# Input projection by seven block products in place of eight, with a short convolution over 1024 tokens

## Chip, cores, metric

The kernel runs on one core of a Trainium2 chip, in float32 throughout. The metric is the device time of one execution in microseconds (us). Engines are named as in the profile: PE (TensorE, matrix products), PEld (its weight loads), DVE (VectorE), ACT (ScalarE), POOL (GpSimd), SP (SyncE, which issues most transfers).

## What is computed

The reference is one layer of a long-convolution mixer and a mixture of experts over 8192 tokens of 512 channels. The part that matters here is its beginning, `x` of [8192, 512] and `W_in` of [512, 1536]:

```python
u = x @ W_in + b_in                              # [8192, 1536]
uc = short_conv(u, short_w, short_b)             # three taps: tokens t-2, t-1, t
x0, x1, v = split(uc, 3)                         # 512 channels each
gate = v * x1
taps = gen_filter(8192, W1, b1, f1, W2, b2, f2, W3, b3)   # small network with sines, times a decay
y = (long_conv(gate, taps) + filter_bias) * x0
x = layernorm(x + y @ W_out + b_out)
# then: experts chosen by a maximum over groups of 32 tokens, two products, layernorm
```

`x` is also read by the projection in a transposed copy, `xT` of [512, 8192].

## The kernel before

There are three stages one after another: `project`, `convolve` and `experts`. Only `project` is changed. It computes `u`, the short convolution and the gate, and beside that the filter's taps, and writes `x0`, `gate` and `taps` to DRAM, from where `convolve` reads them.

The projection works on one block of 512 tokens (`TB`, 16 blocks) and one group of 128 channels (`ct`, four groups) at a time, in `projection(b, ct)`. Its three streams `s` are `x0`, `x1` and `v`. For each stream four matmul calls (over the 512 input channels, `k`) fill one PSUM bank (L260). A call is two records in the profile. ACT then copies the bank to SBUF with the bias added (`u`, L269) and makes the last tap of the short convolution from it (`o`, L271); DVE adds the other two taps (L272, then L277, or for `x0` two halves in another order of tokens, L283). The last two columns of `u` are carried to the next block by two small copies on POOL (L253, L286). POOL multiplies `gate` (L288), and SP stores `x0` (L289) and `gate` (L293).

Between projections stand the pieces of the filter, called `rides`: 16 pieces with sines (`filter_1`, `filter_2`, `sine`, L197 to L203: seven DVE instructions and one of ACT for 512 columns), then 32 pieces that make the taps (`some_taps`: eight small exponentials on ACT at L238, two PSUM adds on DVE at L241, two products on POOL at L245). They are spread evenly over the 64 projections:

```python
upto = len(rides) * (b * NCT + ct + 1) // slots
for f, *args in rides[done:upto]:
    f(*args)
```

PSUM has eight banks, which all these share in turn. Engine orders in this stage are made by the framework's scheduler from the program's order and its modelled durations; a queue then runs its instructions strictly in that order, and semaphores make an instruction wait for what it reads and for the buffer that it writes. Token loads (`load_tokens`, L161) go through SP into two buffers.

Of the kernel before, what the change touches and what calls it, by code (L numbers as in the profile page):

```python
# [13 lines left out]
F32 = mybir.dt.float32  # L14
# [81 lines left out]
@with_exitstack  # L96
def hyena_then_experts(ctx: ExitStack, tc: tile.TileContext, i: dict, out: bass.AP):
    nc = tc.nc

    const = ctx.enter_context(tc.tile_pool(name="const", bufs=1))  # L100
    dram = ctx.enter_context(tc.tile_pool(name="dram", bufs=1, space=bass.MemoryType.DRAM))

    def load(pool, name):
        t = pool.tile(list(i[name].shape), F32, tag=name, name=name + "_sb")
        nc.sync.dma_start(out=t, in_=i[name])
        return t

    ident = const.tile([P, P], F32, tag="ident", name="ident")
    make_identity(nc, ident)

    def in_dram(what, shape):
        return [dram.tile(shape, F32, tag=f"{what}{ct}", name=f"{what}{ct}") for ct in range(NCT)]


    y_dram = {
        (ct, n): dram.tile([P, BT], F32, tag=f"y{ct}_{n}", name=f"y{ct}_{n}")
        for ct in range(NCT)
        for n in range(NBLK)
    }


    with tc.tile_pool(name="pairs", bufs=2) as pairs, tc.tile_pool(name="in", bufs=3) as tables:
        kept = {
            name: const.tile(list(i[name].shape), F32, tag=name, name=name + "_sb")
            for name in ("chan", "c_in", "c_back")
        }
        between = in_dram("x0", [P, L]), in_dram("gate", [P, P, N2]), in_dram("taps", [P, P, N2])
        with tc.tile_pool(name="psum1", bufs=8, space=bass.MemoryType.PSUM) as psum:

            def bank(name):  # L130
                return psum.tile([P, 512], F32, tag="ps", name=name)

            project(tc, i, bank, load, between, kept)
        with tc.tile_pool(
            name="psum2", bufs=4, space=bass.MemoryType.PSUM, reuse_waits="tile"
        ) as psum:

            def banks(name):
                return psum.tile([P, 1024], F32, tag="ps", name=name)

            convolve(tc, i, banks, kept, pairs, tables, between, y_dram)
    experts(tc, i, load, ident, y_dram, out)


def project(tc, i, bank, load, between, kept):


    nc = tc.nc
    x0_dram, gate_dram, taps_dram = between
    with tc.tile_pool(name="pr1", bufs=1) as hp, tc.tile_pool(name="pr2", bufs=2) as wk:  # L150

        win = [hp.tile([P, NCT, 3, P], F32, tag=f"win{ct}", name=f"win{ct}") for ct in range(NCT)]

        def load_win(ct):
            come = i["W_in"].rearrange("(k p) (s t c) -> k t p s c", p=P, s=3, c=P)
            for k in range(NCT):
                nc.sync.dma_start(out=win[ct][:, k], in_=come[k, ct])

        def load_tokens(b):
            xt = wk.tile([P, NCT, TB], F32, tag="xt", name=f"xt_{b}")  # L160
            nc.sync.dma_start(  # L161
                out=xt, in_=i["xT"][:, b * TB : (b + 1) * TB].rearrange("(k p) t -> p k t", p=P)
            )
            return xt


        xt = wk.tile([P, NCT, TB], F32, tag="xt", name="xt_0")
        for k in range(NCT):
            nc.sync.dma_start(
                out=win[0][:, k],  # L170
                in_=i["W_in"].rearrange("(k p) (s t c) -> k t p s c", p=P, s=3, c=P)[k, 0],
            )
            nc.sync.dma_start(out=xt[:, k], in_=i["xT"][k * P : (k + 1) * P, 0:TB])
        pe = load(hp, "pe")
        w1 = load(hp, "W1p")
        w2 = load(hp, "W2p")
        bf = load(hp, "bf")
        chan = kept["chan"]
        nc.sync.dma_start(out=chan, in_=i["chan"])
        for ct in range(1, NCT):  # L180
            load_win(ct)
        w3 = load(hp, "W3p")
        b3 = load(hp, "b3b")
        negt = load(hp, "negt")
# [2 lines left out]
            nc.sync.dma_start(out=kept[name], in_=i[name])  # L187

        h2 = hp.tile([P, L // 2], F32, tag="h2", name="h2")
        carry = hp.tile([P, NCT, 3, 2], F32, tag="carry", name="carry")  # L190
        nc.gpsimd.memset(carry, 0.0)

        def sine(dst, ps, layer, name):
            a = wk.tile([P, 512], F32, tag="a", name="a" + name)
            n = wk.tile([P, 512], F32, tag="n", name="n" + name)
            b_ap, f_ap = bf[:, 2 * layer : 2 * layer + 1], bf[:, 2 * layer + 1 : 2 * layer + 2]
            nc.vector.tensor_scalar(a, ps, b_ap, f_ap, ALU.add, ALU.mult)  # L197
            nc.vector.tensor_scalar(n, a, 1.0 / (2 * math.pi), ROUND, ALU.mult, ALU.add)
# [6 lines left out]
        h1s = {}  # L205

        def filter_1(j):
            ps = bank(f"pf1_{j}")
            nc.tensor.matmul(ps, w1, pe[:, bass.ts(j, 512)], start=True, stop=True)
            h1s[j] = wk.tile([P, 512], F32, tag="h1", name=f"h1_{j}")  # L210
            sine(h1s[j], ps, 0, f"0_{j}")

# [7 lines left out]
        def some_taps(ct, j):  # L220
# [11 lines left out]
                    )  # L232
            for half in range(2):
                n2 = half * N2 // 2 + 4 * j
                ex = wk.tile([P, 4, P], F32, tag="ex", name=f"ex_{ct}_{n2}")
                kb = wk.tile([P, 4, P], F32, tag="kb", name=f"kb_{ct}_{n2}")
                for q in range(4):
                    nc.scalar.activation(  # L238
                        ex[:, q, :], delta[:, chans], AF.Exp, scale=negt[:, n2 + q : n2 + q + 1]
# [8 lines left out]
            if j == N2 // 8 - 1:  # L248
                nc.sync.dma_start(out=taps_dram[ct], in_=taps.pop(ct))

        def projection(b, ct):
            u = wk.tile([P, 3, TB + 2], F32, tag="u", name=f"u_{ct}_{b}")
            nc.gpsimd.tensor_copy(u[:, :, 0:2], carry[:, ct])  # L253
            got = []
            pss = [bank(f"pu_{ct}_{b}_{s}") for s in range(3)]
            steps = [(s, k) for s in range(3) for k in range(NCT)]
            if b == 0 and ct == 0:
                steps.sort(key=lambda sk: sk[1])
            for s, k in steps:
                nc.tensor.matmul(  # L260
                    pss[s], win[ct][:, k, s, :], xt[:, k, :], start=(k == 0), stop=(k == NCT - 1)
                )
            for s in range(3):

                def ch(what):
                    at = (s * NCT + ct) * 5 + what
                    return chan[:, at : at + 1]

                nc.scalar.activation(u[:, s, 2:], pss[s], AF.Identity, bias=ch(0))  # L269
                o = wk.tile([P, TB], F32, tag=f"o{s}", name=f"o{s}_{ct}_{b}")  # L270
                nc.scalar.activation(o, u[:, s, 2:], AF.Identity, bias=ch(1), scale=ch(4))  # L271
                nc.vector.scalar_tensor_tensor(  # L272
                    o, u[:, s, 1 : 1 + TB], ch(3), o, ALU.mult, ALU.add
                )
                first = u[:, s, 0:TB]
                if s:
                    nc.vector.scalar_tensor_tensor(o, first, ch(2), o, ALU.mult, ALU.add)  # L277
                    got.append(o)
                    continue
                got.append(wk.tile([P, 2, TB // N2, N2 // 2], F32, tag="o", name=f"o_{ct}_{b}"))  # L280
                first, o = (v.rearrange("p (a h b) -> p h a b", h=2, b=N2 // 2) for v in (first, o))
                for h in range(2):
                    nc.vector.scalar_tensor_tensor(  # L283
                        got[0][:, h], first[:, h], ch(2), o[:, h], ALU.mult, ALU.add
                    )
            nc.gpsimd.tensor_copy(carry[:, ct], u[:, :, TB : TB + 2])  # L286
            gate = wk.tile([P, TB], F32, tag="gate", name=f"gate_{ct}_{b}")
            nc.gpsimd.tensor_tensor(gate, got[2], got[1], ALU.mult)  # L288
            nc.sync.dma_start(  # L289
                out=x0_dram[ct].rearrange("c (h n) -> c h n", h=2)[:, :, b * TB // 2 : (b + 1) * TB // 2],  # L290
                in_=got[0].rearrange("c h a b -> c h (a b)"),
            )
            nc.sync.dma_start(  # L293
                out=gate_dram[ct][b * TB // N2 : (b + 1) * TB // N2].rearrange("a c b -> c a b"),
                in_=gate.rearrange("c (a b) -> c a b", b=N2),
            )


        rides = []
# [1 line left out]
        for j in range(nf):  # L301
            rides += [(filter_1, j)]
            if j:
                rides += [(filter_2, j - 1)]
        rides += [(filter_2, nf - 1)]
        rides += [(some_taps, ct, j) for ct in range(NCT) for j in range(N2 // 8)]

        slots = NTB * NCT - 2
        done = 0
        for b in range(NTB):  # L310
            if b:
                xt = load_tokens(b)
            for ct in range(NCT):
                projection(b, ct)
                upto = len(rides) * (b * NCT + ct + 1) // slots
                for f, *args in rides[done:upto]:
                    f(*args)
                done = max(done, upto)


CC = 16
# [659 lines left out]
```

## Time and profile before

| what | value |
|---|---|
| time, median of 3 runs | 2325.26 us (2318.59 to 2327.2) |
| the profiled execution: time, span | 2320.76 us, 2319.0 us |
| mean granted TensorE clock | 0.969 of full speed |
| busy: PE, DVE, ACT, POOL | 2152.6, 1297.3, 823.7, 478.2 us |
| `project`, first matmul to the first of `convolve` | 4.83 to 724.38 us |
| matmul records of L260, weight loads | 1536, of 592 ns at the median; 190 ns |

The busy time of an engine is the union of its instructions' durations. Matmuls are pipelined: the 592 ns of one overlap with the next, so the rate is to be read from the distance of their starts. Idle time of an engine "before" an instruction is put down to what ended it, the releaser. A mean duration that is longer than the median says that some instructions of the group were held up while they ran.

### The profile page before, as it was taken

Reading aid. Unit: us, or ns where it says so; the run is one execution under the profiler, and the core shown is the slowest. Engines: PE = TensorE matmul, PEld = TensorE weight load, DVE = VectorE, ACT = ScalarE, POOL = GpSimd, SP = SyncE. Lnnn points to the kernel's source line nnn. Section 1 sums busy time; section 2 is a strip of 40 time slices with the busy share of each in tenths; the row PEclk is TensorE's granted clock in tenths of the full one; section 3 lists DMA queues with packets and bytes.
Section 4 is the critical chain, followed back from the end, with each engine's and each line's share of the span. In section 5 each row is a group of like instructions: output and inputs, shape, how many; then the busy total and the mean of one; then the engine's idle time right before and its main releaser. Section 6 shows DMA issues by size and latency. Waiting matters only on the chain. (4 is left out here: it accounts for less than half of the span.)

```text
span 2319.0 us, 65860 instructions
## 1 busy us (share of the span) xinstructions
PE 2152.6 (93%) x29664; PEld 1474.7 (64%) x29664; DVE 1297.3 (56%) x1872; ACT 823.7 (36%) x1248; POOL 478.2 (21%) x583
## 2 busy tenths in 40 slices
PE   9999999999999999999999998889988999888765
PEld 3444444444446999999999998355555556555643
DVE  5677544554544553463463463456566666656647
ACT  4444555555553321231321221121343234224433
POOL 1111333333331340250250160211100100110000
PEclk9999999999999999999999999999998999899887
DMA  5222224232414655655564574526654754665373
GB/s 167 68 64 76 70 65 167 87 136 64 141 59 168 204 172 192 194 199 183 184 219 174 165 245 167 154 77 195 216 193 136 230 185 137 194 217 188 118 264 121
DMA packets 197057, 362.62 MB, mean 156 GB/s; under 512 B 79132, under 2 KB 118946, under 8 KB 193698
## 3 DMA queue, kind: packets, MB, share of 16 engines
q1 hardware_dynamic: 194472, 341.63, 45.2%
q10 hardware_dynamic: 2304, 16.78, 1.8%
q8 instruction: 233, 3.82, 0.7%
q14 instruction: 48, 0.39, 0.1%
HBM read 274.47 MB, written 83.89 MB: 155 GB/s over the span
## 5 line engine op out<-in xcount | busy, mean ns | idle before, releaser
L260 PE MATMUL pu<-xt,win 128*128 128x512 f32 x1536 | 673.5, 596 | 4.8 <-DMA xt<-in_xT 4.8
L260 PEld LDWEIGHTS pu<-xt,win 128*128 128x128 f32 x1536 | 289.2, 190 | 363.8 <-issue 355.0
L272 DVE SCALAR_TENSOR_TENSOR o<-u,chan_sb,o 128x512 f32<-128x512 f32 x192 | 144.8, 754 | 289.6 <-ACT o L271 270.6
L554 PE MATMUL po<-wout,yt 128*128 128x512 f32 x512 | 240.7, 614 | 19.4 <-DVE x L558 19.2
L383 PE MATMUL px<-place,tab 128*64 128x128 f32 x4096 | 227.6, 273 | 2.2 <-ACT place L366 1.4
L383 PEld LDWEIGHTS px<-place,tab 128*64 128x64 f32 x4096 | 226.0, 136 | 3.3 <-ACT place L366 2.1
L359 PE MATMUL pa<-c_in_sb,vk 128*64 128x128 f32 x4096 | 224.9, 273 | 2.3 <-ACT place L366 1.6
L359 PEld LDWEIGHTS pa<-c_in_sb,vk 128*64 128x64 f32 x4096 | 223.5, 137 | 3.9 <-ACT place L366 1.8
L552 POOL TENSOR_TENSOR xt<-xt,b_outb_sb 128x512 f32<-128x512 f32 x64 | 82.4, 1288 | 619.9 <-DMA xt<-in_x 581.1
L269 ACT ACTIVATE u<-pu,chan_sb 128x512 f32<-128x512 f32 x192 | 130.6, 680 | 182.8 <-PE pu L260 179.0
L405 POOL TENSOR_TENSOR place<-t,hs 128x256 f32<-128x256 f32 x132 | 94.8, 718 | 470.8 <-DVE hs L403 411.2
L554 PEld LDWEIGHTS po<-wout,yt 128*128 128x128 f32 x512 | 94.4, 194 | 130.1 <-issue 96.1
L717 ACT COPY si<-pi 128x1024 f32<-128x1024 f32 x96 | 93.0, 1012 | 196.6 <-PE pi L708 138.3
L271 ACT ACTIVATE o<-u,chan_sb 128x512 f32<-128x512 f32 x192 | 155.6, 812 | 6.5
L368 DVE COPY place<-pa 128x1024 f32<-128x1024 f32 x64 | 78.3, 1224 | 139.7 <-PE pa L359 135.1
L721 DVE STREAM_TRANSPOSE si<-si 128x2048 f32<-128x2048 f32 x48 | 108.1, 2290 | 85.0 <-ACT si L717 85.0
L366 ACT COPY place<-pa 128x1024 f32<-128x1024 f32 x64 | 64.7, 1012 | 251.8 <-PE pa L359 245.7
L416 PE MATMUL pz<-c_back_sb,place 64*128 64x128 f32 x2048 | 123.6, 284 | 14.8 <-POOL place L405 14.8
L238 ACT ACTIVATE ex<-delta_sb,negt_sb 128x128 f32<-128x128 f32 x256 | 87.6, 390 | 132.9 <-POOL taps L245 132.9
L416 PEld LDWEIGHTS pz<-c_back_sb,place 64*128 64x128 f32 x2048 | 122.8, 199 | 15.8 <-POOL place L405 15.8
L708 PE MATMUL pi<-f,h 32*32 32x128 f32 x6144 | 103.4, 291 | 30.2 <-issue 18.2
L398 ACT COPY hs<-px 128x512 f32<-128x512 f32 x132 | 75.5, 572 | 156.9 <-PE px L383 149.0
(86 smaller groups left out, 2655.9 us busy)
## 6 DMA issues: line engine op xcount, KB each, us to landing
f<-in_f SPq DMA_DIRECT2D x160, 512.0 KB, 5.1
tab<-in_c_mid SPq DMA_DIRECT2D x64, 512.0 KB, 3.8
place<-in_c_out SPq DMA_DIRECT2D x64, 512.0 KB, 5.0
x<-o SPq DMA_DIRECT2D x64, 256.0 KB, 2.4
gate<-gate SPq DMA_DIRECT2D x64, 256.0 KB, 2.6
taps<-taps SPq DMA_DIRECT2D x4, 4096.0 KB, 11.2
vk<-taps SPq DMA_DIRECT2D x32, 512.0 KB, 4.0
vk<-gate SPq DMA_DIRECT2D x32, 512.0 KB, 3.5
```

What stands on the lines that cost most here:

```text
L260: nc.tensor.matmul(pss[s], win[ct][:, k, s, :], xt[:, k, :], start=(k == 0), stop=(k == NCT - 1))
L269: nc.scalar.activation(u[:, s, 2:], pss[s], AF.Identity, bias=ch(0))
L271: nc.scalar.activation(o, u[:, s, 2:], AF.Identity, bias=ch(1), scale=ch(4))
L272: nc.vector.scalar_tensor_tensor(o, u[:, s, 1 : 1 + TB], ch(3), o, ALU.mult, ALU.add)
L359: nc.tensor.matmul(ps[r * 64 : (r + 1) * 64, c * N1 : (c + 1) * N1], vk[:, half * 8 + c, :], cin[:, r, :], start=True, stop=True,)
L383: nc.tensor.matmul(ps[h * 64 : (h + 1) * 64, j, :, r, :], tab[:, g % 2 * KC + j, r * 64 : (r + 1) * 64], both[:, :, g * KC + j, h * 64 : ( ...
L405: nc.gpsimd.tensor_tensor(o[:, 0], t[:, 0], hs[:, 1], ALU.subtract)
L416: nc.tensor.matmul(ps[:, h, c, :], spec[rows, r, c0 + c, :], cback[rows, r].rearrange("p q n -> p (q n)"), start=(r == 0), stop=(r == 1),)
L554: nc.tensor.matmul(ps, got["y"][:, ct, t % 2 * P : (t % 2 + 1) * P], wout[:, ct, :], start=(ct == 0), stop=(ct == NCT - 1),)
L708: nc.tensor.matmul(pss[r // 2][s * T : (s + 1) * T, col : col + P], b.h[rows, at + q, s, u * T : (u + 1) * T], f2[rows, q, s, :], start=Tr ...
L717: nc.scalar.copy(o, pss[rr].rearrange("p (r q d) -> p r d q", r=2, q=4))
L721: nc.vector.transpose(turned[:, d].rearrange("p d g -> p (d g)"), stage[:, d].rearrange("p d e -> p (d e)"),)
```

## The change

Take two channel groups (`m` and `m + 2`), two blocks of 512 tokens and two halves of the 512 input channels. The projection of one stream is then a product of 2 x 2 block matrices. Eight block products do it directly; the Winograd form of Strassen's scheme takes seven, with sums of blocks before and after. The class `Quad` holds one such 2 x 2 product: `p1` and `p2` are the first two block products, `the_others` the five further ones with the additions that combine them. There are 48 quads (8 blocks of 1024 tokens, 2 pairs of groups, 3 streams).

- `sums_of_win` makes the sums of weight blocks, on POOL, once for each of the two pairs. `sum_of_tokens` makes four differences of token blocks for each 1024 tokens: on DVE for the first, on POOL for the others.
- Products 1, 2 and (once more) 5 are copied from PSUM by ACT; five additions a quad read PSUM on DVE; two additions a quad are on POOL.
- `short_convolution` works on 1024 tokens and is written one quad behind the products. With `spare_dve`, in the first 27 quads, the third tap of streams `x1` and `v` is made by ACT into `w` and added by POOL; else by DVE.
- The pieces of the filter are placed anew: the 16 with sines in the first 27 quads, the 32 with taps in the following 19.
- The order of PE's instructions is that of the program in this stage. The first eight weight loads are issued from ACT's queue. Input `pe` of the filter is loaded in eight pieces. Temporary buffers of the filter are taken from a pool that `convolve` uses later.

The core of the diff:

```diff
+        A11, A12, S3, A22, S1, S2, S4 = range(7)
+        win = [hp.tile([P, 7, 3, 2, P], F32, tag=f"win{m}", name=f"win{m}") for m in range(NP)]
...
+        def sums_of_win(m):
+            w, e = win[m], nc.gpsimd
+            e.tensor_tensor(w[:, S1], w[:, S3], w[:, A22], ALU.add)
+            e.tensor_tensor(w[:, S2], w[:, S1], w[:, A11], ALU.subtract)
+            e.tensor_tensor(w[:, S4], w[:, A12], w[:, S2], ALU.subtract)
+            e.tensor_tensor(w[:, S3], w[:, A11], w[:, S3], ALU.subtract)
...
+            for name, h, n in (("12", 0, 1), ("11", 0, 0), ("21", 1, 0), ("22", 1, 1)):
+                got[name] = xq = wk.tile([P, 2, TB], F32, tag="xq", name=f"xq{name}_{b}", bufs=5)
...
+        def sum_of_tokens(b, x, name, e):
+            a, c = {"1": ("12", "11"), "2": ("22", "t1"), "3": ("22", "12"), "4": ("21", "t2")}[name]
+            x["t" + name] = t = wk.tile(
+                [P, 2, TB], F32, tag=f"xs{name}", name=f"xs{name}_{b}", bufs=2 if name == "1" else 1
             )
+            e.tensor_tensor(t, x[a], x[c], ALU.subtract)
...
+        load_win(0, nc.scalar)
...
+            def product(self, name, slot, tokens):
+                ps = bank(f"p{name}{self.nm}")
+                for k in range(2):
+                    nc.tensor.matmul(
+                        ps, win[self.m][:, slot, self.s, k, :], self.x[tokens][:, k, :],
+                        start=(k == 0), stop=(k == 1),
+                    )
+                return ps
+
+            def add(self, dst, ps, half, other):
+                nc.vector.scalar_tensor_tensor(dst, ps, self.ch(half, 0), other, ALU.add, ALU.add)
+
+            def p1(self):
+                nc.gpsimd.tensor_copy(self.u[:, :, 0:2], carry[:, self.m, self.s])
+                nc.scalar.copy(self.c[1][0], self.product("1", A11, "11"))
+
+            def p2(self):
+                c11 = self.c[0][0]
+                nc.scalar.activation(
+                    c11, self.product("2", A12, "21"), AF.Identity, bias=self.ch(0, 0)
                 )
+                nc.gpsimd.tensor_tensor(c11, c11, self.c[1][0], ALU.add)
+
+            def the_others(self):
+                (_, c12), (c21, c22) = self.c
+                nc.vector.tensor_tensor(c12, self.product("6", S2, "t2"), c21, ALU.add)
+                nc.vector.tensor_tensor(c22, self.product("7", S3, "t3"), c12, ALU.add)
+                self.add(c21, self.product("4", A22, "t4"), 1, c22)
+                ps = self.product("5", S1, "t1")
+                self.add(c22, ps, 1, c22)
+                t5 = wk.tile([P, TB], F32, tag="t5", name="t5" + self.nm, bufs=1)
+                nc.scalar.copy(t5, ps)
+                nc.gpsimd.tensor_tensor(c12, t5, c12, ALU.add)
+                self.add(c12, self.product("3", S4, "22"), 0, c12)
+                nc.gpsimd.tensor_copy(carry[:, self.m, self.s], self.u[:, :, 2 * TB : 2 * TB + 2])
...
+                o = wk.tile([P, 2 * TB], F32, tag="o", name=f"o_{half}{q.nm}", bufs=5)
...
+                for d in (1, 0):
+                    if d == 0 and spare_dve:
+                        w = wk.tile([P, 2 * TB], F32, tag="w", name=f"w_{half}{q.nm}", bufs=1)
+                        nc.scalar.activation(
+                            w, u[:, half, 0 : 2 * TB], AF.Identity, scale=q.ch(half, 2)
+                        )
+                        nc.gpsimd.tensor_tensor(o, o, w, ALU.add)
+                        continue
+                    nc.vector.scalar_tensor_tensor(
+                        o, u[:, half, d : d + 2 * TB], q.ch(half, 2 + d), o, ALU.mult, ALU.add
+                    )
...
+        n_quads = NTB // 2 * NP * 3
+        filter_until, taps_until = n_quads * 9 // 16, n_quads - 2
...
+            else:
+                q = Quad(b, m, s, x)
+                q.p1()
+                q.p2()
+            if before:
+                short_convolution(before, j < filter_until)
+            if j == 1:
+                sums_of_win(1)
+            for f, *args in rides[done : rides_until(j)]:
+                f(*args)
+            done = max(done, rides_until(j))
+            q.the_others()
+            before = q
+            if b + 1 < NTB // 2:
+                if r == 1:
+                    nxt = load_tokens(b + 1)
+                if r in (3, 4):
+                    sum_of_tokens(b + 1, nxt, "12"[r - 3], nc.gpsimd)
+                if r == 5:
+                    sum_of_tokens(b + 1, nxt, "3", nc.gpsimd)
+                    sum_of_tokens(b + 1, nxt, "4", nc.gpsimd)
```

## Prediction

> **What bounds the kernel now.** I read the page first (busy time and costliest groups), then the busy time by stretch, the waits of the projection stage, and the timeline of a few microseconds where two engines meet.
>
> The page's first rows: share of the span, instructions, and the groups of the line that changes (busy, mean ns, then idle before).
>
> ```profile
> PE 2152.6 (93%) x29664; PEld 1474.7 (64%) x29664; DVE 1297.3 (56%) x1872; ACT 823.7 (36%) x1248; POOL 478.2 (21%) x583
> ...
> L260 PE MATMUL pu<-xt,win 128*128 128x512 f32 x1536 | 673.5, 596 | 4.8 <-DMA xt<-in_xT 4.8
> ```
>
> 1536 records for 768 matmul calls: each float32 matmul is two records. In the timeline the weight loads of this line read "0.19 ... [0.24 <-issue]", so one record follows another every 0.43 us (0.429 over a long stretch). Busy time by stretch (PE, PEld, DVE, ACT, POOL, each us and count, clock, DMA share, GB/s):
>
> ```profile
> 120.00:240.00 120.00, 120.00 (x277) 51.76 (x276) 90.70 (x137) 53.68 (x74) 22.47 (x32) 1.00 0.24 75
> 240.00:360.00 120.00, 120.00 (x385) 55.66 (x384) 61.37 (x95) 64.91 (x125) 43.78 (x49) 1.00 0.21 63
> 600.00:720.00 120.00, 120.00 (x384) 55.56 (x384) 62.32 (x93) 64.07 (x121) 43.26 (x48) 1.00 0.32 112
> ```
>
> PE is busy for all of the stage at full clock; the others are half idle. The waits of the first 725 us (total, times, longest) agree: the others wait for PE's pace, and PE waits once, at the start.
>
> ```profile
> DVE o L272 <- ACT o L271: 268.8, 126, 5.5
> ACT u L269 <- PE pu L260: 179.0, 110, 3.2
> ...
> PE pu L260 <- DMA xt<-in_xT: 4.8, 1, 4.8
> ```
>
> So the stage, from 4.83 us (first matmul) to 724.38 us (first matmul of the next stage), is 719.6 us of PE: 1536 x 0.429 = 659 us of projection and 60 us of filter and tap matmuls. Now what is near the limit without showing: DVE and POOL. Timeline (start, duration, engine):
>
> ```profile
> 242.73 0.42 DVE L199 TENSOR_SCALAR n<-n 128x512 f32<-128x512 f32 x1
> 242.89 1.38 POOL L288 TENSOR_TENSOR gate<-o,o 128x512 f32<-128x512 f32 x1 [2.47 <-DVE o L277]
> 243.18 3.09 DVE L201 SCALAR_TENSOR_TENSOR a<-n,a 128x512 f32<-128x512 f32 x3
> ...
> 253.48 0.74 DVE L277 SCALAR_TENSOR_TENSOR o<-u,chan_sb,o 128x512 f32<-128x512 f32 x1
> 253.65 1.72 POOL L245 TENSOR_TENSOR taps<-kb,ex 128x512 f32<-128x512 f32 x1 [2.07 <-DVE kb L241]
> 254.14 0.69 DVE L241 TENSOR_TENSOR kb<-pk,b3b_sb 128x512 f32<-128x512 f32 x1
> ```
> ```profile
> L201 DVE SCALAR_TENSOR_TENSOR a<-n,a x48: 683/692/1642, 31.7 to 245.6; 128x512 f32<-128x512 f32 x48
> ```
>
> Three L201 should take 2.08 us; the first stretches to 1.64 us, as it starts inside POOL's L288 and ends about 0.55 us behind it. POOL's L245, alone 1.27 us, takes 1.72 when it starts inside DVE's L277 and ends 1.14 us behind that. DVE's L241, with one operand in PSUM, runs beside it at its usual 0.69. So DVE instructions with both operands in SBUF and POOL instructions exclude each other; PSUM ones do not.
>
> **The change part by part.**
>
> *PE.* 48 quads (8 blocks of 1024 tokens x 2 channel pairs x 3 streams), seven products of two calls: 48 x 7 x 2 = 672 calls, 1344 records. 192 fewer x 0.429 = 82 us less. Filter and tap matmuls stay. PE alone would need 719.6 - 82 = 637 us: 343 in the first 27 quads, which carry the 16 filter pieces (27 x 12.0 + 16 x 1.2), and 294 in the last 21 with the 32 tap pieces (21 x 12.0 + 32 x 1.3).
>
> *Sizes.* POOL two-operand: 0.73 at 256 columns (L405), 1.27 at 512, so 2.35 at 1024 and 1.81 at 768. DVE two-operand in SBUF: 0.48 at 256 (L283 alone), 0.75 at 512, so 1.29 at 1024. ACT from SBUF: 0.39 at 128, 0.81 at 512, so 1.37 at 1024. DVE add from PSUM: 0.68 (L241); with the scalar between 0.68 and 0.81 (L197), I take 0.75.
>
> *ACT.* Three PSUM reads a quad in place of four: 48 x 1.85 = 89; 96 taps of 1024 at 1.37 = 132; 36 further ones for the spared DVE = 49; exponentials and sines 98. Sum 368 us, now 383: never the limit. The first eight weight loads move to ACT's queue: about 0.6 us of issue each, 5 us, over before its first PSUM read.
>
> *DVE.* New: five PSUM adds a quad, 48 x 3.6 = 174. Convolution: 92 of 1024 at 1.29 and 128 of 512 at 0.75 = 215, now 302. Sines, taps, first token sums 115. Sum 503 us, now 426.
>
> *POOL.* New: two 512-column adds a quad (96 x 1.27 = 122), 36 adds of 1024 for the spared DVE (85), 28 token differences (66), 8 weight sums (15). Gates 75, taps 81, copies 18. Sum 462 us, now 220.
>
> *The shared path.* DVE's SBUF-only part is 273 of those 503 us. The Trainium skill ("SBUF — State Buffer", section "SBUF: two separate sides") says that DVE and GpSimd take a port pair as an exclusive lock for the whole instruction. By that rule at full durations 273 + 462 = 735 us must stand in line, more than the stage takes today: slower by 15 us before any imperfection. The rows give less: held for 0.55 of DVE's 0.75 and 1.14 of POOL's 1.27, the rest being start-up that overlaps. For 1024 columns that is 1.09 and 2.22. Sum: DVE 215, POOL 415, together 630 us. The measurement decides, but 630 against PE's 637 is a resource at its limit: 357 held against 343 of PE in the first part, 273 against 294 in the second. I take the rows; the rule's 735 is kept for the range.
>
> *First part.* DVE has 269 us of its own. Some 205 of its instructions need the lock, POOL holds it 63% of the time with 0.9 us left on average: 116 us of waiting. Back-to-back DVE instructions overlap by about 0.08 us (L197 at 240.34 for 0.81, the next at 241.07): 30 less. 269 + 116 - 30 = 355 to 385; I take 370.
> *Second part.* 234 + 112 x 0.6 x 0.75 = 284, less 22: DVE stays under PE's 294. For the coupling I take 300.
>
> *Token differences.* The buffers of t2, t3, t4 are single, so each is made on POOL only after the last quad's product of the old block has read it; the fourth block of tokens lands only after that quad's second product. In that quad POOL also has the two gates. Between 0 and 6 us of PE stall for each of 7 blocks; in the first part it lies beside the lock's wait, in the second I take 3 x 4 = 12.
>
> *Start.* The first product needs what it needs now. But the third kind (p6) needs weight sums of 1.8 us each on POOL, behind the loading of 3.5 MB (first stretch: 197 GB/s, so some 17 us), p7 all four: about 22 us, by which PE has done 6 to 11 us of work. Plus 11.
> *End.* Today DVE waits for the last gate store until 732.12 and PE loses 1.6 us. After, the last quad's two convolutions of 4 x 0.75 and ACT's 1.37 stand behind the last product: plus 3.
>
> *Queues.* Stores halve in number (64 of 256 KB to 32 of 512 KB on each output): SP gains. The filter's input comes in 8 small loads on SP; behind a waiting store one could hold PE up to 8 us, at most 64 us. I take 0: the token loads of today are issued at 27.17 and 50.88, each over 20 us ahead of use. The taps' store (11.2 us to landing) can hold POOL once, where two taps' pieces meet in one quad: 0 to 11, taken 0.
>
> **Sum:** 370 + 300 + 12 + 11 + 3 = 696 against 719.6: 24 us less. The profiled execution took 2320.8 us, so 2297; the median of runs is 4.5 higher: 2301.
>
> **Rivals.**
> (a) *The lock packs well, PE stays the bound.* POOL's work falls into DVE's PSUM adds (174 us) and idle. For: these adds read PSUM and so need no lock, and DVE is only 78% full in the first part. Against: 357 held in 343. 637 + 14 = 651: 69 us less, 2257.
> (b) *The gain is eaten.* Both parts lose another 10 to 20 us to order (a POOL add of 1.27 us behind a 2.35 us one, with DVE's last add waiting): 2314 to 2337, no change.
> (c) *The lock is the bound.* One mechanism: in a quad POOL's 1024-column adds stand in front of the short add that DVE's last add waits for, and each DVE convolution instruction waits a whole POOL one, so the line runs at its held time only 80% of the time. Place: mostly the first 27 quads. The break-even is 719.6 / 48 = 15.0 us a quad; held time is 13.1, so it decides below 87% use. At 80%: 630 / 0.8 = 788, less what PE-bound parts would hide, or the rule's 735 + 14: plus 30 to 65, 2355 to 2390. For: neither engine's queue can pass its head. Against: the held time already assumes today's stretched pairs.
> (d) *It does less than it says:* seven products would show as 1344 records; I see no way around that.
>
> **How the numbers follow.** What a measurement of this kernel can tell from no change is about 0.5%, 11.6 us. Main case (2278 to 2313) 0.33, (a) 0.17, (b) 0.15, (c) 0.35. Faster 0.50, same 0.15, slower 0.35. The likeliest case gives 2301; its own range is 2278 to 2313. Both signs hold much of the chance, so the whole range runs from just inside (a) to the low part of (c): 2260 to 2365.
>
> **What would show it.** 1344 records of the product line at 0.429 us; POOL busy over 460 us in the stage; DVE's SBUF-only groups with means well above 1.29 and 0.75, those from PSUM near 0.7; PE, idle 4.8 us now, with waits for DVE (banks) in the first 27 quads and almost none later; the next stage's first matmul at about 701 us. Wrong if PE idles mostly for DMA (queues), if POOL's means at 1024 columns are far from 2.35, or if the second part is the slower one for its work.

## The result and the profile after

The changed kernel takes 2435.28 us (2432.58 to 2435.94, 4 runs) against 2326.05 us for the kernel before in the same comparison: a ratio of 1.0475, interval 1.0451 to 1.0498. The forecast of 2301 us, faster, was wrong in sign and size. The profiled execution has a span of 2433.6 us.

The page of the changed kernel, in the form of the lines shown of before (L306 is the product line; `xs` are token differences, `xq` tokens as loaded):

```profile
PE 2141.1 (88%) x29472; PEld 1452.3 (60%) x29472; DVE 1485.4 (61%) x1888; ACT 779.3 (32%) x1142; POOL 753.3 (31%) x687
...
L306 PE MATMUL p<-xs,win 128*128 128x512 f32 x768 | 388.2, 657 | 74.2 <-POOL xs L199 46.2
...
L306 PE MATMUL p<-xq,win 128*128 128x512 f32 x576 | 275.8, 626 | 52.2 <-DVE kb L277 37.1
```

768 + 576 = 1344 records, as worked out: PE was given 192 fewer. But in front of these stand 74 and 52 us of idle time, where there were 4.8. Busy time by stretch, for the first 27 quads (to 462 us), and from there to the next stage:

```profile
5.00:462.00 457.00, 388.92 (x788) 158.09 (x788) 330.18 (x338) 152.98 (x181) 264.07 (x181) 0.90 0.23 70
462.00:843.00 381.00, 319.16 (x1101) 143.10 (x1100) 264.03 (x290) 171.93 (x370) 220.58 (x176) 0.95 0.29 101
```

The stage, 719.6 us before, is 838 us long: 118.5 us more, where the prediction had 24 less. PE (first number behind the comma) is no longer busy throughout, at 85% and 84%; yet neither is any other engine: DVE 72% and 69%, POOL 58%, ACT 33% and 45%. No engine is full, and all wait. What comes after has the same instructions: from the next stage's first matmul to its second step (`pa` to `px`) 70.5 us, before 57.8, then 658 and 659, and the experts 862 and 878. The loss is all in the projection and the seam behind it. The experts are 16 us shorter, though each engine runs the same instructions there in the same order. No run here explains this; it returns in every version with seven products (859 to 867 us), but not in e3 with eight (880), so the totals below flatter the seven products by 11 to 19 us, and the stage times are the ones to compare.

The waits of the first 850 us:

```profile
DVE u L313 <- POOL u L335: 153.1, 47, 13.4
...
ACT t L334 <- DVE u L313: 103.3, 18, 10.8
...
DVE o L379 <- ACT o L368: 46.7, 37, 1.9
PE p L306 <- POOL xs L199: 46.2, 20, 7.3
...
PE p L306 <- DVE kb L277: 37.1, 22, 4.8
```

The largest is in 47 of 48 quads: DVE's last addition (L313) waits for POOL's addition of the fifth product (L335). That one waits for ACT's copy `t5` (L334), and the copy in turn waits for DVE, which reads the same PSUM bank first in the program's order. Groups of the same stretch show the second loss, instructions that last longer than alone:

```profile
L379 DVE SCALAR_TENSOR_TENSOR o<-u,chan_sb,o 128x1024 f32<-128x1024 f32 x92 | 154.4, 1693 | 47.1 <-ACT o L368 46.7
...
L359 DVE SCALAR_TENSOR_TENSOR o<-u,chan_sb,o 128x512 f32<-128x512 f32 x120 | 105.9, 952 | 19.8 <-ACT o L354 19.8
...
L386 POOL TENSOR_TENSOR o<-o,o 128x1024 f32<-128x1024 f32 x32 | 90.1, 2814 | 2.4 <-DVE o L379 2.3
...
L235 DVE SCALAR_TENSOR_TENSOR a<-n,a 128x512 f32<-128x512 f32 x48 | 63.9, 1332 | 0.2
...
L233 DVE TENSOR_SCALAR n<-n 128x512 f32<-128x512 f32 x16 | 21.6, 1347 | 0.1
```

The means are 1.69, 0.95, 2.81, 1.33 and 1.35 us; alone these take about 1.28, 0.75, 2.35, 0.68 and 0.41. Summed over all groups of the stretch, DVE's durations are 630 us where 503 was worked out, POOL's 498 where 462 was. The last line is a rounding of the filter. It reads one SBUF operand and not two, and is stretched all the same.

One quad of the second part in the timeline shows the round from engine to engine:

```profile
549.82 1.61 DVE L313 SCALAR_TENSOR_TENSOR u<-p,chan_sb,u 128x512 f32<-128x512 f32 x2
...
551.52 0.59 ACT L334 COPY t<-p 128x512 f32<-128x512 f32 x1
552.18 1.09 POOL L335 TENSOR_TENSOR u<-t,u 128x512 f32<-128x512 f32 x1 [1.88 <-ACT t L334]
553.31 0.75 DVE L313 SCALAR_TENSOR_TENSOR u<-p,chan_sb,u 128x512 f32<-128x512 f32 x1 [1.88 <-POOL u L335]
...
554.10 1.24 ACT L368 ACTIVATE o<-u,chan_sb 128x1024 f32<-128x1024 f32 x1 [1.99 <-DVE u L313]
...
555.37 4.64 DVE L379 SCALAR_TENSOR_TENSOR o<-u,chan_sb,o 128x1024 f32<-128x1024 f32 x3 [1.31 <-ACT o L368]
```

DVE, ACT, POOL, DVE, ACT, DVE: at each pass one engine stops until the other is done, which costs DVE 1.88 + 1.31 us in this quad. In a quad of the first part the short add stands behind long ones:

```profile
263.35 0.59 ACT L334 COPY t<-p 128x512 f32<-128x512 f32 x1 [2.52 <-DVE u L313]
263.94 2.35 POOL L377 TENSOR_TENSOR o<-o,w 128x1024 f32<-128x1024 f32 x1
...
266.37 2.35 POOL L386 TENSOR_TENSOR o<-o,o 128x1024 f32<-128x1024 f32 x1
268.67 1.10 POOL L335 TENSOR_TENSOR u<-t,u 128x512 f32<-128x512 f32 x1
269.81 0.75 DVE L313 SCALAR_TENSOR_TENSOR u<-p,chan_sb,u 128x512 f32<-128x512 f32 x1 [6.49 <-POOL u L335]
```

Here DVE waited 6.49 us. The copy was done at 263.94, but POOL's queue does the two 1024-column instructions first. Over all 48 quads, the short add of 36 began when ACT's copy ended, with POOL idle before it (80 us of DVE's waiting in front of L313); in the other twelve POOL was still at earlier work in its queue (75 us).

### The profile page after: what moved, and what is told of

Same layout as the page of the kernel before. It is cut to its first block, busy times and chain, and to the rows that moved or that the text cites. A ratio compares the mean times of both kernels' runs of the same rounds, so it can differ in the third digit from the quotient of the medians.

```text
span 2433.6 us, 65560 instructions
## 1 busy us (share of the span) xinstructions
PE 2141.1 (88%) x29472; PEld 1452.3 (60%) x29472; DVE 1485.4 (61%) x1888; ACT 779.3 (32%) x1142; POOL 753.3 (31%) x687
## 5 line engine op out<-in xcount | busy, mean ns | idle before, releaser
L306 PE MATMUL p<-xs,win 128*128 128x512 f32 x768 | 388.2, 657 | 74.2 <-POOL xs L199 46.2
L306 PEld LDWEIGHTS p<-xs,win 128*128 128x128 f32 x768 | 152.2, 208 | 295.5 <-issue 155.4
L306 PE MATMUL p<-xq,win 128*128 128x512 f32 x576 | 275.8, 626 | 52.2 <-DVE kb L277 37.1
L306 PEld LDWEIGHTS p<-xq,win 128*128 128x128 f32 x576 | 109.5, 197 | 208.8 <-issue 111.5
L313 DVE SCALAR_TENSOR_TENSOR u<-p,chan_sb,u 128x512 f32<-128x512 f32 x144 | 107.8, 749 | 163.9 <-POOL u L335 154.9
L379 DVE SCALAR_TENSOR_TENSOR o<-u,chan_sb,o 128x1024 f32<-128x1024 f32 x92 | 154.4, 1693 | 47.1 <-ACT o L368 46.7
L274 ACT ACTIVATE ex<-delta_sb,negt_sb 128x128 f32<-128x128 f32 x256 | 81.4, 390 | 141.0 <-POOL taps L281 139.8
```

The costliest lines, as they stand in the source:

```text
L274: nc.scalar.activation(ex[:, q, :], delta[:, chans], AF.Exp, scale=negt[:, n2 + q : n2 + q + 1])
L306: nc.tensor.matmul(ps, win[self.m][:, slot, self.s, k, :], self.x[tokens][:, k, :], start=(k == 0), stop=(k == 1),)
L313: nc.vector.scalar_tensor_tensor(dst, ps, self.ch(half, 0), other, ALU.add, ALU.add)
L379: nc.vector.scalar_tensor_tensor(o, u[:, half, d : d + 2 * TB], q.ch(half, 2 + d), o, ALU.mult, ALU.add)
```

## Experiments

Two theories stand against each other. *Handover*: the additions pass from DVE to ACT to POOL and back, in every quad, and each pass stops an engine. *Lock*: DVE instructions with two SBUF operands and POOL's exclude each other, and the line in front of that path is the bound. A third is the new frame itself, the 1024-token convolution and the fixed order of PE. In the table, "stage" is the time from the first product matmul to the first matmul of `convolve` in the profiled execution; the times are medians with the ratio to the kernel before of the same comparison.

| kernel | time (us) | ratio [95%] | stage (us) |
|---|---|---|---|
| before | 2326.05 | 1 | 719.6 |
| changed | 2435.28 | 1.0475 [1.0451, 1.0498] | 838.0 |
| e1 fifth product added by DVE | 2355.94 | 1.015 [1.0128, 1.0172] | 763.8 |
| e2 POOL fills, which read nothing (results left out) | 2343.31 | 1.0085 [1.0065, 1.0105] | 753.1 |
| e3 eight products in the new frame | 2323.62 | 0.9989 [0.9971, 1.0006] | 721.0 |
| e4 third tap not spared | 2394.14 | 1.0304 [1.0283, 1.0324] | 800.4 |
| e5 copy first | 2410.82 | 1.0359 [1.0338, 1.0379] | 813.4 |
| e6 = e1 + e4 | 2332.94 | 1.0028 [1.0015, 1.004] | 738.6 |
| e7 joined | 2305.99 | 0.9911 [0.9889, 0.9932] | 713.5 |
| e8 joined, sines on ACT | 2290.76 | 0.9861 [0.9824, 0.9898] | 697.6 |
| e9 joined, POOL fills (results left out) | 2244.65 | 0.9665 [0.9619, 0.9712] | 651.9 |

**e1, the handover taken out**

```diff
-                t5 = wk.tile([P, TB], F32, tag="t5", name="t5" + self.nm, bufs=1)
-                nc.scalar.copy(t5, ps)
-                nc.gpsimd.tensor_tensor(c12, t5, c12, ALU.add)
+                nc.vector.tensor_tensor(c12, ps, c12, ALU.add)
```

> The fifth product is added to c12 by DVE straight from PSUM; ACT's copy t5 and POOL's add of it are gone, so DVE's last add of a quad waits for no other engine. Handover theory (DVE's last add waiting for ACT and POOL, 153 us of DVE idle in the changed kernel): DVE gets 48 x 0.68 = 33 us more work and loses 153 us of waiting, so the stage, 838 us now, falls to about 720 to 750 and the total to 2320 to 2350. Lock theory (DVE and POOL excluding each other is the bound): POOL holds the path for 48 x 1.14 = 55 us less out of 415, and the stage falls by at most that: total 2380 or above.

Measured 79 us less in all, the stage 74 less: just outside the handover theory's 2320 to 2350, far from the lock theory's 2380. DVE took on 33 us of work and still ended earlier. Its groups in e1 (first 760 us) show where the rest of the 120 us went:

```profile
L377 DVE SCALAR_TENSOR_TENSOR o<-u,chan_sb,o 128x1024 f32<-128x1024 f32 x88 | 152.4, 1744 | 49.6 <-ACT o L366 49.1
...
L357 DVE SCALAR_TENSOR_TENSOR o<-u,chan_sb,o 128x512 f32<-128x512 f32 x120 | 123.9, 1101 | 34.3 <-ACT o L352 34.3
...
L313 DVE SCALAR_TENSOR_TENSOR u<-p,chan_sb,u 128x512 f32<-128x512 f32 x141 | 105.4, 747 | 14.5 <-POOL u L324 1.9 <-PE p L306 1.3 <-DVE u L333 0.9
```

The idle time before L313 fell from 162 to 14.5 us, and the convolution's instructions are stretched more than before, 0.95 to 1.10 us: this fits a DVE with less idle time that meets POOL more often. This edit also takes 48 POOL adds from the shared path, so it does not separate the two theories cleanly.

**e2, the lock taken out**

```diff
-                nc.gpsimd.tensor_tensor(gate, gate, o, ALU.mult)
+                nc.gpsimd.memset(gate, 0.5)
+                nc.gpsimd.memset(gate, 0.5)
+                nc.gpsimd.memset(gate[:, 0:TB], 0.5)
```

and the same for the adds of `w` and for POOL's token differences.

> POOL's 1024-column adds, gates and token differences are replaced by constant fills of about the same total duration (two of 1024 and one of 512 columns), which read nothing from SBUF; these results are left out of the computation. If POOL's reading is what shuts DVE out, DVE's groups shrink towards 1.29 (1024 columns) and 0.75 us, about 80 to 110 us of stretching goes, and under the lock theory the total falls to 2330 to 2350. Handover theory: DVE's idle time behind POOL's short add stays, as POOL is as busy as before; the total falls by about half of that at most, 2380 to 2410. If fills shut DVE out as well, nothing changes.

Measured 92 us less, inside the lock theory's range. A wait and groups of e2:

```profile
DVE u L318 <- POOL u L340: 151.4, 48, 8.3
...
L386 DVE SCALAR_TENSOR_TENSOR o<-u,chan_sb,o 128x1024 f32<-128x1024 f32 x92 | 128.5, 1411 | 49.1 <-ACT o L373 48.7
...
L382 POOL MEMSET o<- 128x1024 f32 x36 | 34.5, 958 | 32.0 <-DVE o L386 32.0
...
L240 DVE SCALAR_TENSOR_TENSOR a<-n,a 128x512 f32<-128x512 f32 x48 | 32.5, 677 | 0.2
```

The filter's L240 (L235 of the changed kernel) falls from 1.33 to 0.68 us, its time alone, though POOL is nearly as busy (its durations sum to 481 us, in the changed kernel to 498) and 32 of the 48 ran beside a fill. So for these two-operand instructions it is POOL's reading of SBUF that shuts DVE out. L386 keeps 1.41 us, because POOL's tap products and short adds still read SBUF; the 20 that met only fills took 1.28. The one-operand roundings are another matter: in e9, which has the same fills, four of them met nothing but fills and took 0.65 to 1.58 us, against 0.41 alone. DVE still waits 151 us for the short add, as the handover theory said: the two losses are separate in kind. One reservation: a fill does not wait for ACT's `w`, for loaded tokens or for the second operand of a gate, so e2 also lost those waits (35 us of POOL's for `w` alone).

**e3, the frame alone**

```diff
+            def output(self, half, n):
+                ps = bank(f"p{half}{n}{self.nm}")
...
+                nc.scalar.activation(self.c[half][n], ps, AF.Identity, bias=self.ch(half, 0))
```

> The new frame (1024-token convolution one quad behind, new placing of the filter's pieces, PE in program order, third tap spared as in the changed kernel) with eight plain block products accumulated in PSUM in place of seven: no sums of weights or tokens, no additions after the products, four copies with bias by ACT. If the additions of the seven-product scheme are what costs (handover and lock both), this one is bound by PE again: stage 659 + 60 = 720 us, total 2320 to 2340. If the new convolution and order are at fault, it stays near 2400 or above.

Measured 2323.62 us, ratio 0.9989 with 1 inside the interval. The stage is PE-bound again, as PE's group (8.3 us of idle time) and the waits of e3 show:

```profile
L320 PE MATMUL p<-xq,win 128*128 128x512 f32 x1536 | 673.3, 597 | 8.3 <-DMA win<-in_W_in 5.2 <-DMA xq<-in_xT 3.1
...
ACT u L324 <- PE p L320: 181.3, 100, 4.0
```

Beside eight products the 1024-token convolution and the fixed order cost nothing. The loss belongs to the seven products' additions and sums. (This version also has eight token buffers in place of five.)

**e4, the third tap not spared**

```diff
-                short_convolution(before, j < filter_until)
+                short_convolution(before, False)
```

> In the first 27 quads DVE makes the third tap itself (36 more instructions of 1024 columns, 46 us) and POOL's 36 adds of 1024 columns and ACT's 36 products go. Lock theory: POOL holds the path for 80 us less, DVE for 39 more, and POOL's short adds stand behind fewer long ones: the total falls by 20 to 40, to 2395 to 2415. A theory in which DVE's own work is the bound: the total rises by up to 46, to 2480. Handover theory: DVE's waits behind POOL in the first part (up to 13 us each) shrink, against 46 us more work: no change within 15 us.

Measured 41 us less, one microsecond outside the lock theory's range. Giving DVE 46 us more work made the kernel faster. On the path, a 1024-column add on POOL costs 2.21 us, the DVE instruction that it spares 1.08 (in the changed kernel's trace, by how long after the other engine's instruction a waiting one ends). But the queue got shorter too: DVE's wait for the short add fell from 153 to 127 us, and e4 does not tell the two apart.

**e5, the order of two lines**

```diff
                 ps = self.product("5", S1, "t1")
-                self.add(c22, ps, 1, c22)
                 t5 = wk.tile([P, TB], F32, tag="t5", name="t5" + self.nm, bufs=1)
                 nc.scalar.copy(t5, ps)
                 nc.gpsimd.tensor_tensor(c12, t5, c12, ALU.add)
+                self.add(c22, ps, 1, c22)
```

> Only the order of two lines is changed: ACT's copy t5 of the fifth product and POOL's add of it stand ahead of DVE's add of the same bank, so the copy waits for PE and no longer for DVE (the changed kernel's ACT waits 103 us there). Every instruction stays; the lock's work is the same. Handover theory: ACT's copy and POOL's add run beside DVE's earlier adds, most of the 153 us of DVE idle goes, stage 838 falls by 60 to 100 us, total 2335 to 2375. Lock theory: POOL and DVE need the path as long as before, total 2420 to 2435.

Measured 24 us less: both ranges missed, the handover theory's by more. The waits of e5:

```profile
DVE u L313 <- POOL u L334: 68.7, 29, 13.2
...
DVE u L313 <- ACT t L333: 57.1, 19, 7.3
```

153 us became 126: now DVE waits for ACT's copy, which in ACT's queue may stand behind work that itself waits for DVE (ACT's first taps wait 139 + 74 us for DVE here), and for POOL, whose queue holds the long instructions. The order in which the bank is read is worth 24 us. That the rest of the handover comes of the queues of ACT and POOL is the likely reading, and no run isolates it.

**e6, both**

> The fifth product added by DVE from PSUM, and the third tap made by DVE in all quads. Alone the two gave 79 and 41 us. If handover and lock are two separate losses the gains add up: stage about 720, total 2310 to 2325, the level of the kernel before. If they are two faces of one (DVE late), the second gives little on top: 2340 to 2360, as DVE's own work is now 503 + 33 + 46 = 582 us.

Stage 738.6: 99 us less than the changed kernel, where the parts alone gave 74 and 38. They nearly add up. The total of 2332.94 lies between the two expectations, 8 us above the range for separate losses and 7 below the other.

**e7, two waits more**

```diff
-            for half in range(2):
+            for half in (1, 0):
...
-                got[name] = xq = wk.tile([P, 2, TB], F32, tag="xq", name=f"xq{name}_{b}", bufs=5)
+                got[name] = xq = wk.tile([P, 2, TB], F32, tag="xq", name=f"xq{name}_{b}", bufs=6)
...
+                sums("2")
```

(`sums` makes t2, t3, t4 right behind the product that read the old ones; the tokens are also loaded one quad earlier.)

> As the one before, and two waits more are taken out: the convolution takes the second channel half first, whose input is ready before DVE's last add (DVE waits 47 + 20 us for ACT's first tap in the changed kernel), and the token differences t2, t3, t4 are emitted right behind the last product that reads their buffer, with a sixth buffer for the tokens so that their input is there (PE waits 46 us for them). Handover theory: another 40 to 80 us, stage 650 to 690, total 2255 to 2290, below the kernel before. If DVE's work and the lock are what is left, under 20 us on top of the one before.

Measured 27 us less than e6, between the two expectations, and the first version with the whole computation whose total is below that of the kernel before clear of the noise. Its stage is shorter by 6 us. The seam is 7 us longer than before, so most of what the total gains comes with the shorter experts (865 us). DVE's waits for ACT's first tap fell to 9 + 11 us, PE's for the token differences only from 46 to 28. Busy time by stretch in e7 (PE, PEld, DVE, ...):

```profile
200.00:300.00 100.00, 94.83 (x211) 40.43 (x210) 97.17 (x114) 30.61 (x36) 45.30 (x30) 0.95 0.23 69
...
400.00:500.00 100.00, 92.06 (x342) 43.29 (x342) 83.52 (x97) 52.15 (x114) 60.60 (x48) 0.99 0.36 122
```

DVE is 97% busy in this stretch, and 98% in those of 100 us on either side of it (79% in the first 100 us): the handover is gone, and DVE's own time with the stretching is the likely bound there.

**e8, work moved from DVE to ACT**

```diff
-            nc.vector.tensor_scalar(a, ps, b_ap, f_ap, ALU.add, ALU.mult)
-            nc.vector.tensor_scalar(n, a, 1.0 / (2 * math.pi), ROUND, ALU.mult, ALU.add)
-            nc.vector.tensor_scalar(n, n, ROUND, None, ALU.subtract)
+            nc.scalar.activation(a, ps, AF.Identity, bias=bfp[:, layer : layer + 1], scale=f_ap)
+            nc.scalar.activation(n, a, AF.Identity, bias=rnd[:, 0:1], scale=1.0 / (2 * math.pi))
+            nc.scalar.activation(n, n, AF.Identity, bias=rnd[:, 1:2])
```

> The joined version with three of the seven DVE instructions of each filter piece (shift and scale, and the two roundings) made by ACT, which is 37% busy. In the joined version DVE is busy 97% of the first 400 us. If DVE's time, its own and the stretching, is what sets the end there, 16 x (0.81 + 0.42 + 0.42) = 26 us of it and the 14 us of stretching on the two roundings go: stage 20 to 40 us shorter, total 2265 to 2290. If PE's waits for the token differences and the banks set it, under 10 us.

Stage 16 us shorter, total 15: a little less than was expected if DVE is the bound, and more than if it is not. At 2290.76 us it is the fastest version with the whole computation, 1.4% below the kernel before. Of the 27.6 us between the two spans 21.9 lie in the stage and 11 in the experts, and the seam takes 6 back. So some 16 us, 0.7%, can be put down to the projection and its seam.

**e9, the lock taken out of the joined version**, with the fills of e2.

> The joined version with POOL's gates and token differences replaced by fills of about the same duration that read nothing (these results are left out). It measures what the exclusion still costs there: DVE's groups in the joined version are about 107 us longer than alone. If that sets the end, stage 713 falls to 650 to 670 and the total to 2240 to 2260; if DVE's own work or PE's waits do, total 2285 or above.

Measured 2244.65 us, inside the lock theory's range, stage 651.9. Groups and a stretch of e9:

```profile
L365 DVE SCALAR_TENSOR_TENSOR o<-u,chan_sb,o 128x512 f32<-128x512 f32 x120 | 89.1, 815 | 7.1 <-ACT o L360 7.1
...
L240 DVE SCALAR_TENSOR_TENSOR a<-n,a 128x512 f32<-128x512 f32 x48 | 33.0, 687 | 0.7
```
```profile
100.00:400.00 300.00, 300.00 (x762) 132.99 (x761) 282.40 (x366) 107.09 (x148) 137.99 (x164) 1.00 0.27 83
```

PE is busy for all 300 us at full clock again, though DVE is 94% busy. 652 us is what the prediction's case (a) gave for a PE-bound stage (637 + 14). So once the handovers are out, POOL's reading is what separates the seven products from their full gain: 62 us. This holds the exclusion together with the waits that a fill does not have, for loaded tokens and for a gate's second operand; PE's own waits for token differences fell from 28 to 2 us with it, and the two are not told apart.

## Why the prediction was wrong

- *PE's share was right.* 1344 records, and a stage of 652 us in e9, where PE is the bound again, against 651.
- *The lock's size was about right.* Over both parts 116 + 50 = 166 us of DVE waiting were reckoned, less 52 for overlap; DVE's durations grew by 127. The held times for 1024 columns were right too: 1.08 us on DVE (median of 37 cases) and 2.21 on POOL (one case) in the changed kernel, against 1.09 and 2.22. The 735 us for whole instructions and the 630 from the rows both lie below the 838 measured, so neither was the term that failed. The Trainium skill, page "SBUF — State Buffer", section "SBUF: two separate sides", also says that a DVE instruction with two SBUF inputs is shut out only by a GpSimd instruction that reads SBUF: e2 agrees (0.68 us beside fills; 1.33 on average in the changed kernel, where some meet adds).
- *The step that failed is the sums "First part" (370) and "Second part" (300).* They took DVE as always having work, so that only the lock made it wait, and left 15 us above the sum of 355 in the first part and 6 us for the coupling in the second. The first stretch measured 457 us from the first matmul, against 370 + 11 with the start; the second 381 against 312. DVE was busy for only 330 and 264 us of them. In place of the coupling stands its idle time: 153 us for POOL's short add (73 in the first part, 80 in the second) and 47 + 20 for ACT's first tap. In e7, where little of this is left and DVE makes the third tap, the stage is 713.5 us.
- *The ledger of the additions was wrong in kind.* ACT's copy of the fifth product was costed as work beside DVE's. In the program it comes behind DVE's read of that bank and waits for it (ACT's 103 us). A sum of busy times cannot show this; the order of the lines and the semaphores can. e5 puts the order alone at 24 us.
- *Rival (c) had the right sign and a part of the mechanism,* the short POOL add behind long ones with DVE's last add waiting. At 0.35 it had a larger chance than the main case, 0.33, which the prediction calls the likeliest. Its price, 30 to 65 us of total, was at most 60% of the 109 measured: it had the path used at 80%, and 630 us held in a stage of 838 is 75%. Its place was wrong. At the old 15.0 us a quad the first 27 quads lost 52 us and the last 21 lost 66, and in 18 of these 21 the short add had no POOL work in front and waited for the copy.
- *The third tap on POOL was counted as relief for DVE.* By the prediction's own held times (2.22 against 1.09) it loads the path, and without it e4 is 41 us faster.
- *Smaller terms. Token differences:* PE waited 11.7 us for them in the second part, where 12 was taken, but 34.5 in the first, where the prediction put them beside the lock's wait. *Banks:* PE's waits for DVE's tap adds (37 us) all fall in the second part, where almost none was expected. *End:* 3 us taken, 12.7 measured between the first two steps of the next stage. *Start:* the sixth product of the first quad began at 20 us, near the 17 to 22 reckoned. *Queues:* taken at 0; the waits show no loss for the filter's small loads.

## What to carry to other kernels

When work is moved off a full engine onto three others, count the passes from engine to engine in one unit of work and the queue that each lands in, not only the busy sums: here PE was 85% busy, DVE, ACT and POOL were below 75%, and the stage was 16% longer. Count DVE's two-SBUF-operand instructions and POOL's as one resource before moving an add to POOL; here an add read from PSUM by DVE was cheaper than a copy by ACT and the same add on POOL, although DVE was the busier engine. A cheaper algorithm pays only when its additions fit beside the products: the seven products took 1.4% off the total with fewer handovers (0.7% in the projection and its seam), and added 4.7% with more.

## What was not expected of the hardware

PE's granted clock fell in the stage to 0.90 and 0.95 (the last columns but two of the stretches above); before it was 1.00 there. In the trace's record of the clock the low stretches are at half clock and last 3.4 us or a multiple, 136 us of the stage together. Product matmuls that start in them follow each other at 0.85 us, where 0.43 is the full rate; the distances of 0.5 to 0.95 us there come to some 33 us more than at full clock. The half-clock time goes with PE's idle time: 102 us in e5, 75 in e1, 34 in e7, 14 in e9, none in e3 and before. So an idle PE pays twice. The Trainium skill ("TensorE: Matmul & The Clock Gate", Part 1) gives a window of 3.4 us for this gate, and the trace's stretches agree with it. How much of the 118 us this is was not separated: in e9 the clock returns to 1.00, in the stretch shown, together with everything else.
